# A two-layer graph network on one core: the self part of pass 1's operands turned on VectorE and reloaded, operand products in one batch, moments on ScalarE

## The chip, the core and the metric

The kernel runs on one core of a Trainium2 chip. The metric is the device time of one execution in microseconds. A core has five engines, each with its own instruction queue, which it works off in order: TensorE (PE in the profile; its weight loads are shown apart as PEld), VectorE (DVE), ScalarE (ACT), GpSimd (POOL) and SyncE (SP), which here issues nearly all DMAs. Engines wait for one another by semaphores. Matmuls write to PSUM, eight banks of 2 KB a partition; everything else lies in SBUF.

## The reference

128 graphs of 64 nodes with 768 features pass through two layers, both with a layer norm and a ReLU ahead and a residual sum behind.

```python
# layer 0
h = relu(layernorm(x))
ctx  = (adj @ (h @ Wadj.T + badj)) / deg + (adj.T @ (h @ Wrev.T + brev)) / rdeg + h @ Wself.T + bself
rel  = einsum('bij,bijr->bir', adj, E[rels]) @ Wr.T + br * deg     # here rels = heads = adj
rel += einsum('bij,bijr->bir', adj.T, E[rr]) @ Wrr.T + brr * rdeg
x = x + ctx + rel
# layer 1: graph attention with six heads and a gate
h = relu(layernorm(x))
x = x + gat(h, adj)
```

The relation part is computed as a count of ids in each row, times a small table.

## The kernel before

Two graphs make a tile of 128 rows and two tiles a pair: 32 pairs. Pass 1 computes layer 0 for all pairs, pass 2 layer 1. Everything named below is pass 1 unless it says otherwise. All arithmetic is float32, but for the counts, which are exact in bfloat16.

**Products.** The three dense products of a pair, h normed by the adjacency, by its transpose, and h itself, each by its own 768 x 768 weight, are one product with a contraction of 3 x 768. Rows (2 tiles, `k`), contraction (3 blocks, `q`) and columns (3 blocks) are multiplied by a scheme that needs 15 block products (`PRODUCTS`) where the plain way needs 18 (`PLAIN`, used in pair 0). Its left factors are the operands `a{k}{q}` and their sums `f1` to `f11` (`A_SUMS`), its right factors weight blocks and their sums (`B_SUMS`), which stay in SBUF all through pass 1. A block product is six matmuls of 128 x 128 by 128 x 256: two blocks of 128 (`q`) times three parts (`s`: adjacency, reverse, self). `main` lists these matmuls as steps: 90 for a pair, and one for the last count product. A product ends with an add or subtract of its PSUM bank on VectorE into the x tile (L630, L632), after a product of counts for some (L622). There are four accumulator banks, `pwa` to `pwd`; a bank goes on accumulating after it has been read, so its next product waits for VectorE's read.

**Operands.** `operands(p, k, q)` (L582) makes the transposed left factors of one pair for one `k` and `q`: eight rows of it in the trace are four float32 matmuls with h (64 rows of one graph, 128 columns) as the stationary and `rts` (64 x 192) as the moving side. `rts` holds the scaled adjacency, the scaled transpose, and a third part that is the identity: it turns h without change. Each call fills two banks of the `pb` pool (two buffers of two banks), and ScalarE copies the result to an `op` tile of 128 x 768 (L599). `form` (L602) makes the sums on VectorE.

**Order.** All queues are written out by hand. `merged` walks through the steps of pair p and puts in the side work of `beside(p)` where its number says: the operands of pair p+1 in three batches of two calls (46, 58, 70), its norm (`deviation` L280, `scaled_mean`, `relu`, at 13 and 20), degrees, counts of ids (`ids_worth`, `ids_sum`, `digits`), the sums of operands, the loads of x for p+2 (66), and the end of pair p-1. That end, `finish`, has three parts for each tile: moments of the new x on VectorE; relu, residual sum on POOL, and two stores; transpose in 32 x 32 blocks on VectorE and a store. Pass 2 reads this last store back in 128-byte pieces in such a way that it arrives transposed (`load_h`, L329).

**The seam.** In the last pair `fetch` (L338) loads the weights of layer 1 over those of layer 0 as these come free, loads h of pair 0 (step 30), and makes the weight sums on VectorE. The ends of the last pair are put into the first round of pass 2 (L1203).

Of the kernel before, what the change touches and what calls it, by code (L numbers as in the profile page):

```python
# [15 lines left out]
P = 128  # L16
# [57 lines left out]
               "+", i > 0) for i, q in enumerate((0, 2, 1)) for k in range(2) for j in range(3))  # L74

# [55 lines left out]
def kernel(  # L131
# [86 lines left out]

    H1D = [[dram.tile([KB * P, P], F32, name=f"h1_{p}_{k}") for k in range(2)] for p in range(NP)]
# [52 lines left out]
    def row_constants():  # L272
        nc.sync.dma_start(bb, row(b_att, P))
        nc.vector.tensor_scalar(bb, bb, 1.0, None, op0=OP.add)
        for c in range(3):
            for i in range(NPART):
                a = c * HB + i * H
                nc.sync.dma_start(dl[a : a + H, :], ident[0:H, 0:H])

    def deviation(src, to, mv):  # L280

        st = small.tile([P, 2, 6], F32, name="st")
        for i in range(2):
            nc.vector.bn_stats(st[:, i, :], src[:, i * HALF : (i + 1) * HALF])
        nc.vector.bn_aggr(mv, st.rearrange("p a b -> p (a b)"))
        ve = small.tile([P, 1], F32, name="ve")
        nc.vector.tensor_scalar(ve, mv[:, 1:2], EPS, None, op0=OP.add)  # L287
        nc.gpsimd.tensor_tensor(to[:, 0:1], ve, mhalf, op=OP.pow)  # L288

# [48 lines left out]
    def fetch():  # L338


        def load_block(n):
            j, q = int(n[1]), int(n[2])
            to = bw2[n].rearrange("p (k s n) -> p k s n", k=KQ, s=2)
            for s, src in enumerate((w_cat, hw_t)):
                nc.sync.dma_start(
                    to[:, :, s, :],
                    src.rearrange("(j k p) n -> j p k n", k=KQ, p=P)[j][:, :, q * CQ : (q + 1) * CQ])

        return ([(30, lambda: load_h(0)), (67, lambda: nc.sync.dma_start(hbb, row(hb, P)))]
                + [(i, lambda n=n: load_block(n)) for i, n in (  # L350
                    (7, "b10"), (13, "b00"), (13, "b21"), (25, "b11"), (31, "b01"), (37, "b20"),
                    (49, "b22"), (49, "b02"), (61, "b12"))]
                + [(i, lambda n=n: sum_of_weights(bw2, n)) for i, n in (
                    (22, "g10"), (28, "g6"), (41, "g12"), (46, "u"), (50, "g14"), (57, "w"),
                    (59, "g5"), (65, "v"), (67, "g3"), (70, "g9"), (73, "g1"), (76, "g8"),
                    (79, "g11"))])


    with ExitStack() as px:
# [123 lines left out]
        H0, ADF, AB, CNT, CT_T, GR, WO, SUM, HF = {}, {}, {}, {}, {}, {}, {}, {}, {}  # L483
# [5 lines left out]

        def prep(p):  # L490

            af = ADF[p] = work.tile([P, 2, 2, N], F32, name="af", bufs=1)
            nc.vector.tensor_copy(af, AI[p])
            ab = AB[p] = work.tile([P, 2, 2, N], BF16, name="ab", bufs=1)
            nc.vector.tensor_copy(ab, af)
# [86 lines left out]
        def operands(p, k, q):  # L582


            t = 2 * p + k
            ps = pss.tile([P, GT, 512], F32, name="pb")
            for i in range(2):
                kb = 2 * q + i
                for g in range(GT):
                    s = slice(g * N, (g + 1) * N)  # L590
                    nc.tensor.matmul(ps[:, g, i * 3 * N : (i + 1) * 3 * N],  # L591
                                     H0[t][s, kb * P : (kb + 1) * P],
                                     rts[p % 2][s, k].rearrange("p s n -> p (s n)"),
                                     start=True, stop=True)

            a = OPS[p, f"a{k}{q}"] = (
                work.tile([P, KQ, 3, P], F32, name="oq") if (k, q) == (1, 1) else
                work.tile([P, KQ, 3, P], F32, name="op", bufs=17))
            nc.scalar.copy(a.rearrange("p h s (g n) -> p g (h s) n", g=GT),  # L599
                           ps[:, :, : 6 * N].rearrange("p g (x n) -> p g x n", n=N))  # L600

        def form(p, *names):  # L602

            for n in names:
                s0, x, s1, y = A_SUMS[n]
                t = OPS[p, n] = work.tile([P, KQ, 3, P], F32, name="op", bufs=17)
                signed(t, s0, OPS[p, x], s1, OPS[p, y])

        def main(p):
# [4 lines left out]
            def new(b):  # L614
                bank[b] = psw.tile([P, 512], F32, name=f"pw{b}")
# [18 lines left out]
            def product(an, bn, b, first, c, sign, cnt):  # L634
                def step(q, s):
                    if first and q == s == 0:
                        new(b)
                    nc.tensor.matmul(  # L638
                        bank[b][:, :CQ], OPS[p, an][:, q, s, :],
# [23 lines left out]
        def finish(p, k):  # L663
# [4 lines left out]
            def norm_and_store():  # L668
                scaled_mean(to, mv)
                h = HF[t] = keep.tile([P, D], F32, name="hf", bufs=3)  # L670
                nc.scalar.activation(h, X[t], AF.Relu, scale=to[:, 0:1], bias=to[:, 1:2])  # L671
                nc.gpsimd.tensor_add(X[t], X[t], h)  # L672
                nc.sync.dma_start(of[t * P : (t + 1) * P, :], X[t])
                hh = keep.tile([P, D], F32, name="hh", tag="hf", bufs=3)
                nc.scalar.activation(hh, h, AF.Identity, scale=0.5, bias=half)
                nc.sync.dma_start(HHD[p][k * P : (k + 1) * P, :], hh)

            def turn_and_store():


                ht = keep.tile([P, D], F32, name="ht", tag="hf", bufs=3)
                nc.vector.transpose(ht, HF[t])
                nc.sync.dma_start(H1D[p][k].rearrange("(b p) n -> p b n", p=P),
                                  ht.rearrange("p (b n) -> p b n", b=KB))

            mv = small.tile([P, 2], F32, name="mv")
            return (lambda: deviation(X[t], to, mv), norm_and_store, turn_and_store)
# [31 lines left out]
        operands(0, 0, 0)  # L719
# [3 lines left out]
        operands(0, 0, 1)  # L723
# [3 lines left out]

        def devs(p):
            DEV[p] = deviations((2 * p, 2 * p + 1))

        def relus(p):
            for k in range(2):
                mean_and_relu(2 * p + k, DEV[p][0][k], DEV[p][1][k])

        def degrees_and_norms(p):
            rd = degrees(p)
            relus(p)
            one_over(rd)
            over_degrees(p, rd)

        def weights_sums(*names):
# [7 lines left out]
            (4, lambda: operands(0, 0, 2)),  # L749
            (8, lambda: count(0, 1)),  # L750
            (12, lambda: operands(0, 1, 0)),
            (12, lambda: operands(0, 1, 1)),
            (17, lambda: operands(0, 1, 2)),
# [16 lines left out]
            (54, lambda: operands(1, 1, 2)),  # L770
            (54, lambda: operands(1, 1, 1)),
# [3 lines left out]
            (64, lambda: operands(1, 0, 0)),  # L775
            (64, lambda: operands(1, 0, 2)),
# [3 lines left out]
            (80, lambda: operands(1, 1, 0)),  # L780
            (80, lambda: operands(1, 0, 1)),
# [4 lines left out]
        def beside(p):  # L786


            ends = [f for k in range(2) for f in finish(p - 1, k)]
            steps = [(0, lambda: form(p, "f5", "f6", "f3")), (10, lambda: form(p, "f10")),  # L790
                     (18, lambda: form(p, "f11"))]
            steps += list(zip((32, 40, 44, 49, 55, 59), ends))
            if p == 1:
                steps += [(8, lambda: weights_sums("g9")), (25, lambda: weights_sums("g1"))]
            if p == 3:
                steps += [(74, row_constants)]
            if p + 1 == NP:
                return steps + fetch()
            n = p + 1
            return steps + [  # L800
                (7, lambda: prep(n)),
                (13, lambda: devs(n)),
                (20, lambda: degrees_and_norms(n)),
                (30, lambda: prep_c(n)),
                (37, lambda: ids_worth(n, 0)),
                (43, lambda: ids_sum(n, 0)),
                (46, lambda: operands(n, 1, 2)),
                (46, lambda: operands(n, 1, 1)),
                (53, lambda: form(n, "f1")),
                (56, lambda: ids_worth(n, 1)),  # L810
                (58, lambda: operands(n, 0, 0)),
                (58, lambda: operands(n, 0, 2)),
                (61, lambda: ids_sum(n, 1)),
                (64, lambda: digits(n)),
                (66, lambda: form(n, "f7", "f4")),
                (66, lambda: load(n + 1)),
                (70, lambda: operands(n, 1, 0)),
                (70, lambda: operands(n, 0, 1)),
                (77, lambda: form(n, "f8", "f9", "f2")),
                (80, lambda: count_t(n, 0)),  # L820
                (85, lambda: count_t(n, 1))]

        for p in range(NP):
# [4 lines left out]
    with ExitStack() as px:  # L828
# [374 lines left out]
        ends = [f for k in range(2) for f in finish(NP - 1, k)]  # L1203
        order = parsed(ORDER)
        SUMMED_HERE = (NT - 1,)
        for i in range(min(k for _, k in order), NP - 2):
            if i >= 0:
                load(i + 1)
            for j, (n, k) in enumerate(order):
                if i == 0 and j in (33, 56, 62, 78, 100, 106):  # L1210
                    ends.pop(0)()
# [53 lines left out]
```

## Time and profile before

| | |
|---|---|
| time, median of 3 runs (2452.13 to 2452.39) | 2452.14 us |
| the profiled execution | 2452.42 us |
| its span | 2450.6 us |
| TensorE busy | 2424.8 us |
| VectorE busy | 2047.8 us |
| ScalarE busy | 1025.6 us |
| POOL busy | 449.2 us |
| HBM read, written | 96.07 MB, 100.66 MB |

The page has one line an engine, then the span in 40 slices, then DMA queues, the chain of work that ended last, and the costliest groups of instructions: line, engine, operation, output<-inputs, shapes, count, then busy time, mean of one, and the idle time ahead of them with what ended it. The slices of TensorE, VectorE and the DMA engines show pass 1 in the first 24 and pass 2 after them:

```profile
PE   9999999999999999999999998999999999999997
DVE  8888788788788788788788767789999989888999
DMA  5112212212213113113113146565555555555544
```

In pass 1 a pair repeats every 45.74 us: the transpose of counts of a pair's second tile stands at 803.53 us in the timeline of TensorE and that of the next pair at 849.27. Records of matmuls overlap in the trace, so what a stretch of them takes is read from their starts.

### The profile page before, as it was taken

To read this page: it belongs to the slowest core of one execution; us is meant where nothing else is said; L and a number is where in the kernel's file an instruction comes from. 1 tells how busy PE (TensorE), PEld (TensorE's weight loads), DVE (VectorE), ACT (ScalarE), POOL (GpSimd) and SP (SyncE) were. 2 spreads that over 40 slices of the span, in tenths; PEclk is the share of its full clock that TensorE was granted. 3 is DMA by queue.
4 is the path that set the end of the run, shared out by engine and by line. 5 is a ranking of instruction groups with operands and counts; after the bars stand their busy time and mean duration, and the time that the engine had idled before them with its cause. 6 is when DMAs were issued, how large, how long until landed. Compare 5 with 4: busy or idle time off the path is not lost.

```text
span 2450.6 us, 34880 instructions
## 1 busy us (share of the span) xinstructions
PE 2424.8 (99%) x11777; PEld 1689.8 (69%) x11777; DVE 2047.8 (84%) x4169; ACT 1025.6 (42%) x3399; POOL 449.2 (18%) x799
## 2 busy tenths in 40 slices
PE   9999999999999999999999998999999999999997
PEld 7888888888888888888888885444444444444445
DVE  8888788788788788788788767789999989888999
ACT  2122222222222222122122122776777777777677
POOL 1112112112112112112122112111111111111122
PEclk9999999999999999999999999999999999999999
DMA  5112212212213113113113146565555555555544
GB/s 181 55 54 90 73 54 92 70 55 95 67 54 99 64 54 102 60 54 108 55 55 108 54 115 161 91 119 116 113 109 113 113 108 115 108 107 118 109 98 101
DMA packets 348660, 224.54 MB, mean 92 GB/s; under 512 B 236234, under 2 KB 298813, under 8 KB 348482
## 3 DMA queue, kind: packets, MB, share of 16 engines
q1 hardware_dynamic: 338610, 197.51, 30.0%
q0 software_dynamic: 9728, 24.78, 6.4%
q8 instruction: 92, 1.51, 0.2%
q14 instruction: 86, 0.70, 0.1%
q10 hardware_dynamic: 144, 0.04, 0.0%
HBM read 96.07 MB, written 100.66 MB: 80 GB/s over the span
## 4 chain that ended last, share of the span: by engine, by line
PE 93%; DVE 4%; ACT 1%; DMA 1%; issue 0%; SPq 0%; DVEq 0%; POOL 0%; ACTq 0%; POOLq 0%
PE pwa L638 20%; PE pwb L638 16%; PE pma L908 13%; PE pmb L908 11%; PE pwc L638 7%; PE pwd L638 7%; PE pb L591 6%; PE pmc L908 4%; PE pmd L908 4%; PE ps L1061 2%; PE pwd L622 1%; PE ps L1043 1%; DVE weights L309 1%; ACT pr L960 1%; PE ps L1012 0%
## 5 line engine op out<-in xcount | busy, mean ns | idle before, releaser
L638 PE MATMUL pwa<-weights,op 128*128 128x256 f32 x2304 | 547.7, 382 | 4.1 <-DVE x L630 2.6
L638 PEld LDWEIGHTS pwa<-weights,op 128*128 128x128 f32 x2304 | 420.8, 190 | 66.9 <-issue 7.6
L638 PE MATMUL pwb<-weights,op 128*128 128x256 f32 x1536 | 360.8, 381 | 0.3 <-DVE x L630 0.3
L638 PEld LDWEIGHTS pwb<-weights,op 128*128 128x128 f32 x1536 | 286.6, 190 | 44.4 <-issue 6.7
L908 PE MATMUL pma<-weights,op_f 128*128 128x512 f32 x620 | 310.3, 597 | 1.1 <-DVE weights L935 0.8
L288 POOL TENSOR_TENSOR rn<-ve,mhalf 128x1 f32<-128x1 f32 x128 | 93.5, 730 | 935.4 <-DVE ve L287 935.3
L309 DVE TENSOR_TENSOR op<-op 128x768 f32<-128x768 f32 x248 | 241.4, 993 | 1.2
L960 ACT ACTIVATE pr<-pr 128x128 f32<-128x128 f32 x768 | 225.3, 295 | 25.1 <-DVE pr L950 24.1
L488 ACT ACTIVATE h<-x,rn 128x768 f32<-128x768 f32 x64 | 62.4, 1020 | 383.1 <-DVE rn L292 364.2
L671 ACT ACTIVATE hf<-x,rn 128x768 f32<-128x768 f32 x64 | 65.7, 1027 | 357.6 <-DVE rn L292 349.3
L908 PEld LDWEIGHTS pma<-weights,op_f 128*128 128x128 f32 x620 | 112.2, 190 | 138.7 <-issue 103.2
L599 ACT COPY op<-pb 128x768 f32<-128x768 f32 x160 | 121.1, 797 | 180.0 <-PE pb L591 179.8
L908 PE MATMUL pmb<-weights,op_f 128*128 128x512 f32 x372 | 193.1, 601 | 0.4 <-DVE hz L935 0.4
L638 PE MATMUL pwc<-weights,op 128*128 128x256 f32 x780 | 187.0, 383 | 0.0
L638 PE MATMUL pwd<-weights,op 128*128 128x256 f32 x768 | 176.3, 379 | 0.0
L638 PEld LDWEIGHTS pwc<-weights,op 128*128 128x128 f32 x780 | 145.6, 190 | 25.2 <-issue 6.7
L672 POOL TENSOR_TENSOR x<-x,hf 128x768 f32<-128x768 f32 x64 | 135.7, 2121 | 133.4 <-ACT hf L671 133.4
L638 PEld LDWEIGHTS pwd<-weights,op 128*128 128x128 f32 x768 | 145.8, 190 | 20.0 <-issue 0.2
L591 PE MATMUL pb<-r,h 64*128 64x192 f32 x1536 | 152.0, 337 | 0.4 <-ACT h L488 0.4
L591 PEld LDWEIGHTS pb<-r,h 64*128 64x128 f32 x1536 | 123.0, 187 | 33.9 <-issue 23.0
L960 ACT ACTIVATION_READ_ACCUMULATOR pr<-pr 128x1 f32 x768 | 144.3, 188 | 0.0
L1033 ACT ACTIVATE pb<-al,mx 128x64 f32<-128x64 f32 x384 | 128.5, 337 | 12.4 <-DVE mx L1025 11.6
(210 smaller groups left out, 4143.6 us busy)
## 6 DMA issues: line engine op xcount, KB each, us to landing
x<-in_x_dram SPq DMA_DIRECT2D x64, 384.0 KB
out_dram<-x SPq DMA_DIRECT2D x64, 384.0 KB
hh<-hh SPq DMA_DIRECT2D x64, 384.0 KB
h<-ht SPq DMA_DIRECT2D x64, 384.0 KB
h<-h SPq DMA_DIRECT2D x256, 96.0 KB
x<-hh SPq DMA_DIRECT2D x64, 384.0 KB
out_dram<-f POOLq DMA_DIRECT2D x62, 384.0 KB, 4.7
hx<-weights SPq DMA_DIRECT2D x88, 192.0 KB
```

The lines of the kernel that those rows point to most:

```text
L288: nc.gpsimd.tensor_tensor(to[:, 0:1], ve, mhalf, op=OP.pow)
L309: return (nc.vector.tensor_add if s1 == "+" else nc.vector.tensor_sub)(to, x, y)
L488: nc.scalar.activation(h, X[t], AF.Relu, scale=to[:, 0:1], bias=to[:, 1:2])
L591: nc.tensor.matmul(ps[:, g, i * 3 * N : (i + 1) * 3 * N], H0[t][s, kb * P : (kb + 1) * P], rts[p % 2][s, k].rearrange("p s n -> p (s n)"), ...
L599: nc.scalar.copy(a.rearrange("p h s (g n) -> p g (h s) n", g=GT), ps[:, :, : 6 * N].rearrange("p g (x n) -> p g x n", n=N))
L638: nc.tensor.matmul(bank[b][:, :CQ], OPS[p, an][:, q, s, :], bw[bn][:, (s * KQ + q) * CQ : (s * KQ + q + 1) * CQ], start=(first and q == s ...
L671: nc.scalar.activation(h, X[t], AF.Relu, scale=to[:, 0:1], bias=to[:, 1:2])
L672: nc.gpsimd.tensor_add(X[t], X[t], h)
L908: nc.tensor.matmul(bank[p, b], operand(p, an)[:, q, :], bw2[bn][:, 2 * q * CQ : 2 * (q + 1) * CQ], start=(first and q == 0), stop=(q == KQ ...
L960: nc.scalar.activation(PR[t][:, j, h, :], PR[t][:, j, h, :], AF.Copy, accum_out=to)
L1033: nc.scalar.activation(PB[t][:, h, :], AL[t][:, h, :], AF.Exp, bias=MX[t][:, h : h + 1], accum_out=DN[t][:, h : h + 1])
L1061: nc.tensor.matmul(po[r][o, c, :], PT[t][s, c, o], (hs if r == g else HX[t])[s, 2 * c + r, :], start=True, stop=True)
```

## The change

Nothing changes in the 15 products, the counts or pass 2's own work. Seven things change in pass 1:

1. For pairs from 2 on (`SHARED`) the self part of an operand is not made by a matmul. ScalarE writes the normed h once more with its columns mixed (`relu_mixed`), VectorE transposes it in 32 x 32 blocks (`turn_own`), SP stores it to DRAM (`put_own`), and six DMAs load it transposed into the third part of the operand tiles (`load_own`). The operand matmuls have 128 columns instead of 192, and ScalarE copies 512 elements a partition instead of 768.
2. The six calls of a pair come in one batch (`operands_in_one`) at step 83, over six banks: both `pb` buffers and the banks of c and d, which now are one tile.
3. The moments of these norms and of all ends are two passes on ScalarE with accumulators (`moments`) and three small instructions on POOL (`norm_of`), where two statistics instructions, an aggregate, an addition and a scaled mean ran on VectorE.
4. The casts of the adjacency are on ScalarE, from pair 1 on.
5. Operand tiles have fixed places (`SLOTS`), two sums are made in place (`IN_PLACE`), and their layout has the part outside the block.
6. The side work of `beside` is in smaller pieces in the new order `BESIDE`: f4, f8, f9 and f2 are made in the pair that uses them, loads of the self part stand ahead of the stores of the pair before, and loads of x behind these.
7. At the seam the loads of h of pair 0 move from step 30 to step 62.

```diff
+BESIDE = {"f5": 1, "prep": 1, "dev0": 5, "f4": 8, "dev1": 11, "f8": 12, "deg": 15, "f9": 16,
+          "norm0": 16, "turn0": 17, "f2": 18, "f3": 18, "f6": 19, "put0": 20, "f10": 21,
+          "f11": 25, "norm1": 25, "edev0": 25, "over": 28, "turn1": 32, "enorm0": 32,
+          "rts": 34, "put1": 36, "eturn0": 36, "a11": 38, "a00": 40, "a01": 42, "prepc":
+          43, "esum0": 43, "a12": 45, "a02": 46, "etput0": 49, "edev1": 51, "idw0": 54,
+          "ids0": 54, "idw1": 58, "ids1": 60, "eput0": 62, "enorm1": 62, "esum1": 62,
+          "eput1": 62, "load": 62, "dig": 65, "a10": 70, "ct0": 71, "eturn1": 79, "ct1":
+          82, "etput1": 83, "ops": 83, "f1": 85, "f7": 86}
...
+    def moments(src, by):
+        sums = small.tile([P, 2], F32, name="su")
+        nc.scalar.activation(by, src, AF.Copy, scale=-1.0 / D, accum_out=sums[:, 0:1])
+        nc.scalar.activation(by, src, AF.Square, bias=sums[:, 0:1], accum_out=sums[:, 1:2])
+        return sums
+
+    def norm_of(sums, to):
+        nc.gpsimd.tensor_scalar(to[:, 0:1], sums[:, 1:2], 1.0 / D, EPS, op0=OP.mult, op1=OP.add)
+        nc.gpsimd.tensor_tensor(to[:, 0:1], to[:, 0:1], mhalf, op=OP.pow)
+        nc.gpsimd.tensor_tensor(to[:, 1:2], sums[:, 0:1], to[:, 0:1], op=OP.mult)
...
-        return ([(30, lambda: load_h(0)), (67, lambda: nc.sync.dma_start(hbb, row(hb, P)))]
+        return ([(62, lambda: load_h(0)), (67, lambda: nc.sync.dma_start(hbb, row(hb, P)))]
...
+        def relu_mixed(t, to):
+            hp = HP[t]
+            nc.scalar.activation(
+                hp.rearrange("p (b f i) -> p b f i", b=KB, f=NQ),
+                X[t].rearrange("p (b i f) -> p b f i", b=KB, f=NQ),
+                AF.Relu, scale=to[:, 0:1], bias=to[:, 1:2])
+
+        def turn_own(t):
+            h = HPT[t] = work.tile([P, D], F32, name="hpt", bufs=1)
+            nc.vector.transpose(h, HP[t])
+
+        def put_own(t):
+            nc.sync.dma_start(H0D[t].rearrange("(b p) n -> p b n", p=P),
+                              HPT[t].rearrange("p (b n) -> p b n", b=KB))
...
+        def load_own(p, *names):
+            for n in names:
+                k, q = int(n[1]), int(n[2])
+                nc.sync.dma_start(
+                    new_operand(p, n)[:, 2].rearrange("p b (a n) -> p (b a) n", a=NQ),
+                    H0D[2 * p + k].rearrange("(b i) (f n) -> (i f) b n", i=Q, n=Q)[
+                        :, q * KQ * NQ : (q + 1) * KQ * NQ, :])
...
-        def operands(p, k, q):
-            t = 2 * p + k
-            ps = pss.tile([P, GT, 512], F32, name="pb")
...
+        def operands(p, *calls, last=False):
+            n = 2 if p in SHARED else 3
+            if last:
+                CD.clear()
+                ps = psw.tile([P, GT, 512], F32, name="pwcd")
+            else:
+                ps = pss.tile([P, GT, 512], F32, name="pb")
...
+        def operands_in_one(p):
+            calls = ((1, 2), (1, 1)), ((0, 0), (0, 2)), ((1, 0), (0, 1))
+            ps = [operands(p, *c, last=c is calls[2]) for c in calls]
+            for v, c in zip(ps, calls):
+                operands_out(p, v, *c)
...
+        SHARED = range(2, NP)
...
+                if n in IN_PLACE:
+                    OPS[p, n] = OPS[p, IN_PLACE[n]]
+                else:
+                    new_operand(p, n)
+                signed(OPS[p, n], s0, OPS[p, x], s1, OPS[p, y])
...
-                        bank[b][:, :CQ], OPS[p, an][:, q, s, :],
+                        bank[b][:, :CQ], OPS[p, an][:, s, q, :],
```

In `beside`, a name with `dev`, `norm`, `turn` or `put` belongs to the norm of pair p+1, one with an `e` ahead of it to the end of pair p-1, a name `a..` is a load of a self part, `idw`, `ids`, `dig` and `ct` are the counts, and `ops` is the batch. In the first round of pass 2 the ends of the last pair are put in at the same places as before, with the moments on ScalarE.

## The prediction

> **What bounds the kernel now.** I read the page first (busy shares, the chain of waits, the costly groups), then the busy time by windows, then TensorE's timeline around one batch of operand products, and last the seam between the passes.
>
> ```profile
> PE 2424.8 (99%) x11777; PEld 1689.8 (69%) x11777; DVE 2047.8 (84%) x4169; ACT 1025.6 (42%) x3399; POOL 449.2 (18%) x799
> ...
> PE 93%; DVE 4%; ACT 1%; DMA 1%; issue 0%; SPq 0%; DVEq 0%; POOL 0%; ACTq 0%; POOLq 0%
> ...
> L591 PE MATMUL pb<-r,h 64*128 64x192 f32 x1536 | 152.0, 337 | 0.4 <-ACT h L488 0.4
> ```
>
> The chain is TensorE for 93% of the span. In pass 1 TensorE never idles (the columns are length, then PE, PEld, DVE, ACT, POOL busy):
>
> ```profile
> 600.00:800.00 200.00, 200.00 (x1079) 169.42 (x1078) 161.25 (x326) 50.55 (x72) 39.70 (x37) 1.00 0.25 83
> ```
>
> So pass 1 lasts as long as its matmul stream, and busy VectorE time counts only where TensorE would wait for it. A busy sum overlaps itself (a record of 382 ns starts every 216 ns), so I take times from starts. One batch of two calls of `operands` inside product b:
>
> ```profile
> 824.77 1.89 PE L638 MATMUL pwb<-weights,op 128*128 128x256 f32 x8
> 826.59 1.57 PE L591 MATMUL pb<-r,h 64*128 64x192 f32 x16
> 828.09 1.13 PE L638 MATMUL pwb<-weights,op 128*128 128x256 f32 x4
> 829.06 2.75 PE L638 MATMUL pwd<-weights,op 128*128 128x256 f32 x12
> ```
>
> Twelve records of L638 take 2.59 us (829.06 to the next row, 831.65), 0.216 each; a float32 matmul is two records, so a step of the main list is 0.432 us. From 824.77 to 829.06 are 4.29 us, 2.59 of them the twelve records of L638: the batch costs 1.70 us. Pair 0 has a smaller batch beside a full one:
>
> ```profile
> 17.09 0.92 PE L591 MATMUL pb<-r,h 64*128 64x192 f32 x8
> 17.94 3.72 PE L638 MATMUL pwa<-weights,op 128*128 128x256 f32 x16
> 21.59 1.57 PE L591 MATMUL pb<-r,h 64*128 64x192 f32 x16
> 23.09 2.43 PE L638 MATMUL pwa<-weights,op 128*128 128x256 f32 x10
> ```
>
> Eight more records take 1.50 - 0.85 = 0.65 us, 0.163 for each two: the halves g = 0 and 1 sit on different rows of the array and run together. Sixteen are 8 x 0.163 = 1.30 us, so 0.40 us of each batch goes into changing to 64 rows and back. What 128 columns on 64 rows take is seen in pass 2 (L1061):
>
> ```profile
> 1816.07 0.28 PE L1061 MATMUL ps<-hx,pT 64*64 64x128 f32 x2
> 1816.08 0.36 PE L1061 MATMUL ps<-weights,pT 64*64 64x128 f32 x2
> 1816.17 0.28 PE L1061 MATMUL ps<-hx,pT 64*64 64x128 f32 x2
> ```
>
> A group follows a group after 0.10 to 0.11 us. At the seam VectorE is the bound for a moment:
>
> ```profile
> 1447.12 2.86 PE L638 MATMUL pwa<-weights,op 128*128 128x256 f32 x12 [0.29 <-DVE x L630]
> ...
> 1481.47 4.54 PE L638 MATMUL pwa<-weights,op 128*128 128x256 f32 x12 [2.33 <-DVE x L630]
> ...
> 1490.35 2.86 PE L638 MATMUL pwa<-weights,op 128*128 128x256 f32 x12 [1.52 <-DVE x L632]
> ```
>
> **What the Trainium skill says.** "TensorE: Matmul & The Clock Gate", The mechanism: matmuls of different row groups run at once, and weight loads overlap those of other groups; the trace agrees (0.163 us for two). The same page, LDWEIGHTS: a load takes its columns over 1.2 GHz, whatever the rows; 128 columns are then 107 ns. "TensorEngine Tiling (Array Packing)", Key Properties: a change of tiling mode drains the array; the 0.40 us is what this trace shows of it. "DMA: Bandwidth & Descriptors", Two DMAs through the same engine are not ordered: a reload has to wait for the store's semaphore. No run shown has that in pass 1, but the turned h of layer 1 goes the same way.
>
> **The change part by part.** *Operand products.* For pairs 2 to 31 the columns fall from 192 to 128 and three batches become one: 48 records, 24 twos. Per two, the moving side gives 0.108 (L1061). The load: 187 ns for 128 columns here, 132 for 64 columns in L1061, so 55/64 ns a column, 110 ns for 128 plus a fixed part that overlaps. I take 0.110. New batch 24 x 0.110 + 0.40 = 3.04 us against 3 x 1.70 = 5.10: 2.06 us a pair, 30 pairs, 61.8 us. Bounds: 0.107 gives 64; a load that doesn't overlap, 0.187, gives 24 x 0.187 + 0.40 = 4.89, and 6 us in all. Pairs 0 and 1 keep 192 columns: nothing.
>
> *The batch's own waits.* It begins before step 83 of 91; call that 0. Its third group needs banks c and d, whose last adds come after steps 71 and 53: free. ScalarE's copies fall from 768 to 512 elements a partition (0.80 us now; 640 elements fewer, the copies of L580 at 0.27, give 0.83 ns an element, so 0.59). The first group is ready at about 1.3, six copies end at 4.9; the last count product, in bank d, comes at 3.04 + 7 x 0.432 + 2 x 0.22 = 6.5. Then f7 is wanted at 6.7. On VectorE it is last in a row: the add of product 13 (ready at 3.04 + 0.43 + 0.22 + 0.2 = 3.9, 0.42), f1 and f7 (0.99 each by the page's L309) end at 6.3. Covered, by 0.4 us, the least cover of the new order. f4, f8, f9 and f2, moved behind the start of their own pair, have 3 us and more.
>
> *VectorE.* Per pair go four deviations (two 0.55, 0.21, 0.15, 0.15 us each, 6.4 in all) and two casts (0.58); two transposes come (0.97 each). It gets 5 us lighter. Its densest stretch is steps 54 to 78: four products and sums of ids (2.04 + 1.88, twice), digits 1.0, and between them the adds of f6 and f8. From the add of f11 at 24.1 us of the pair, f6's add ends at 30.8 (wanted at 32.1) and f8's at 33.8 (wanted at 34.7): 0.9 us of cover, so nothing on the path. If that goes, what is late is the b bank of product 13.
>
> *ScalarE and POOL.* The moments add two ScalarE passes to each of four tiles (1.02 us and up to 0.19 for the accumulator, as in L960), the mixed relu two: 12 us a pair beside 12 now, in 43.7: hidden. POOL gets three small instructions (0.73 each, L288) where it had one. The wait this makes is that of the transpose of h (`turn0`, step 17) on moments, POOL and relu: ScalarE reaches `dev0` about 1.1 us before the pair begins, so 1.3, 3.5 after POOL, 4.8 after the mixed relu. VectorE gets there at 8.1 anyway. Queued behind it are f2 and f3, and f3 is wanted at 13.3 and done at 11.2: cover 3.3 + 2.1 = 5.4 us.
>
> *DMA.* A pair stores 2 x 384 KB more and loads 6 x 128 KB in 128-byte pieces; 73 GB/s (400 to 1400 us) over 45.7 us are 3.3 MB now, so 4.9 MB in 43.7 us, 112 GB/s. Pass 2 runs at 111 GB/s with such pieces and TensorE full. On SP the loads of a11, a00, a01, a12 and a02 wait for the second store (issued at about 17.5 us of the pair) and for PE at step 41; they should land near 25, and f1 asks at 41. The x loads stand behind the pair's stores, at about 29, and are read after 42. Hidden.
>
> *The seam.* In the last pair, h of pair 0 (eight DMAs, 4.86 us of SP at 1458.42) no longer stands ahead of the weights b01 and b20, and the stores no longer wait for VectorE's moments. So VectorE's weight sums come some 4 us sooner and no longer pile up at 1478 to 1490. There now go 2.33 + 1.52 us of waiting and 4.54 - 2.75 = 1.8 us of a slower clock after it. I take 4 of these 5.6 us; the unknown (later h loads, four more forms in this pair) makes it 7 gained to 3 lost.
>
> **Sum.** 61.8 + 4 = 66 us. The profiled execution took 2452.42, with a span of 2450.6; the median of the runs is 2452.14, so one sum serves both: 2386 us.
>
> **The rivals.** *A, a thin cover at f7.* VectorE's forms beside POOL have reached 1.1 us in the trace's rows (839.88, two in 2.17), which takes most of the 0.4; with later copies TensorE waits 0.4 us a pair: 12 us back, 2398. For it: the cover is small. Against: before, the same kind of chain never stopped TensorE.
>
> *B, loads don't overlap.* 187 ns for two: only 6 + 4 us gained, 2442. For it: loads and products become equally long, which no batch here shows. Against: the present two take 163 ns with a load of 187.
>
> *C, slower: VectorE stands at the transpose of h.* In order, it holds f2, f3 and all adds behind. The moments are not in this trace. Each us beyond the 5.4 of cover stops TensorE in 30 pairs; past 5.4 + 2.2 = 7.6 us the gain is gone. Nine us late would be 3.6 x 30 = 108 lost, 2494. For it: three engines in a row and x loads behind stores. Against: nothing in the sums above comes near.
>
> That the change does nothing would need pass 1 to be bound by something else, which the full windows exclude.
>
> **How the numbers follow.** Forecast 0.76 (own range 2377 to 2396), A 0.10, B 0.05, C 0.06, 0.03 that gains and waits cancel. The range 2376 to 2404 takes in A. Faster (by over 0.2%, 5 us, what such a measurement can tell) 0.91, same 0.03, slower 0.06.
>
> **What would show it.** Starts of like rows one pair apart (45.74 us now) at about 43.7; L673 rows of 48 records in 2.9 us; no wait of TensorE on VectorE above 0.3 us in steady pairs; the gaps at the seam mostly gone. Rows of L673 at 0.19 a two would mean B, waits at the first L745 rows of a pair A, long VectorE idle before the transpose of `hp` C.

## The result, and the profile after

The changed kernel takes **2620.23 us** (median of 4 runs, 2619.53 to 2622.63) against 2452.17 us for the kernel before beside it: a ratio of 1.0687, with a 95% interval of 1.0668 to 1.0705. It is slower by 168 us; the forecast was 66 us faster. The profiled execution has a span of 2617.8 us and a mean granted TensorE clock of 0.958, as a share of full speed (0.998 before).

The page of after, with busy times, the slices of TensorE and its clock, and the chain that ended last:

```profile
PE 2456.4 (94%) x11777; PEld 1720.5 (66%) x11777; DVE 1988.0 (76%) x3547; ACT 1335.0 (51%) x4017; POOL 520.3 (20%) x1047
...
PE   7999899989989998999899899999999999999997
...
PEclk8999999989998999999899999999999999999999
...
PE 81%; DVE 14%; ACT 1%; DMA 1%; issue 1%; POOL 1%; SPq 0%; DVEq 0%; POOLq 0%; ACTq 0%
```

VectorE's busy time fell and ScalarE's rose, as meant. But VectorE's share of the chain went from 4% to 14%, and in pass 1 both TensorE and its clock have slices below 9. The same 200 us as in the prediction (length, then PE, PEld, DVE, ACT, POOL busy, then PEclk):

```profile
600.00:800.00 200.00, 182.94 (x958) 155.49 (x957) 136.95 (x216) 79.93 (x138) 41.44 (x58) 0.93 0.35 98
```

TensorE, full before, now stands still for 17 of the 200 us, at a mean clock of 0.93. What it waits for, from the waits of TensorE over the whole span (sum, times, longest):

```profile
PE pb L652 <- POOL c L644: 126.9, 30, 4.3
PE pwcd L745 <- DVE x L737: 12.7, 1, 12.7
```

L652 is the transpose of a pair's counts, L644 the copies on POOL that it reads; L745 is a product of the main list, L673 an operand product, L729 a product of counts. One wait in TensorE's timeline, and the batch of operand products behind it:

```profile
830.27 2.32 PE L745 MATMUL pwcd<-weights,op 128*128 128x256 f32 x10
836.86 0.47 PE L652 MATMUL pb<-identb,c 128*126 128x128 bf16 x2 [4.27 <-POOL c L644]
837.13 1.17 PE L745 MATMUL pwcd<-weights,op 128*128 128x256 f32 x2
838.09 0.63 PE L729 MATMUL pwcd<-tab,cntT 126*128 126x256 bf16 x2
838.51 4.97 PE L745 MATMUL pwa<-weights,op 128*128 128x256 f32 x12
...
845.16 0.65 PE L745 MATMUL pwb<-weights,op 128*128 128x256 f32 x2
845.74 2.06 PE L673 MATMUL pb<-r,h 64*128 64x128 f32 x32
847.63 1.06 PE L673 MATMUL pwcd<-r,h 64*128 64x128 f32 x16
848.62 0.70 PE L745 MATMUL pwb<-weights,op 128*128 128x256 f32 x2
849.15 0.39 PE L729 MATMUL pwb<-tab,cntT 126*128 126x256 bf16 x2
```

Three things are to be seen (a product of the main list is twelve records). Ten records from 830.27 end at 832.43 (0.216 each), so the transpose, at 836.86, is 4.43 us late. Then twelve records take 4.81 us (838.51 to the next row at 843.32) instead of 2.59: TensorE runs at about half speed for a while after the wait, called the half clock from here on. And the batch itself costs what was forecast: from 845.16 to 849.15 are 3.99 us, less four records of L745 at 0.216 leaves 3.13 us (3.04 forecast). The steady pair, from one batch to the next, is 51.20 us, against 45.74 before.

Why the copies on POOL are late, from VectorE's timeline of the same pair:

```profile
825.29 0.42 DVE L737 TENSOR_TENSOR x<-pwcd,x 128x256 f32<-128x256 f32 x1 [1.36 <-PE pwcd L729]
825.63 1.01 DVE L616 TENSOR_TENSOR eq<-gr,vals 128x1664 bf16<-128x1664 bf16 x1
826.68 2.52 DVE L619 TENSOR_TENSOR eq<-eq,wo 128x1664 bf16<-128x1664 bf16 x1
829.23 1.89 DVE L624 TENSOR_REDUCE sum<-eq 128x26 f32<-128x1664 bf16 x1
831.15 1.02 DVE L616 TENSOR_TENSOR eq<-gr,vals 128x1664 bf16<-128x1664 bf16 x1
832.21 1.02 DVE L619 TENSOR_TENSOR eq<-eq,wo 128x1664 bf16<-128x1664 bf16 x1
833.15 0.42 DVE L737 TENSOR_TENSOR x<-pwa,x 128x256 f32<-128x256 f32 x1
833.49 1.88 DVE L624 TENSOR_REDUCE sum<-eq 128x26 f32<-128x1664 bf16 x1
...
836.04 0.25 DVE L639 CAST cnt<-di 128x156 bf16<-128x156 int32 x1
836.20 0.41 DVE L739 TENSOR_TENSOR x<-x,pwb 128x256 f32<-128x256 f32 x1
```

and from POOL's:

```profile
825.69 2.63 POOL L781 TENSOR_TENSOR x<-x,hf 128x768 f32<-128x768 f32 x1 [1.14 <-ACT hf L777]
836.42 0.72 POOL L644 COPY c<-cnt 128x243 bf16<-128x243 bf16 x2 [8.10 <-DVE cnt L639]
```

The work on ids of both tiles (two comparisons L616, two products L619, two sums L624) and the digits behind it form one row from 825.63 to 836.2, with one add out of PSUM in it. POOL waits 8.10 us for their end. And the first L619 took 2.52 us where the second took 1.02: it stood beside the residual add on POOL (825.69 to 828.32). So the theory (**T** in the expectations): TensorE waits for counts because their transpose came forward into a stretch of VectorE that ends later than it, and each wait is followed by the half clock. The rivals: something else in the new order also holds TensorE, so that the time stays up when this wait goes (**R**), or the clock falls for another reason.

### The profile page after: what moved, and what is told of

Read it like the earlier page. It is cut to its first block, busy times and chain, and to the rows that moved or that the text cites. A ratio compares the mean times of both kernels' runs of the same rounds, so it can differ in the third digit from the quotient of the medians.

```text
span 2617.8 us, 35645 instructions
## 1 busy us (share of the span) xinstructions
PE 2456.4 (94%) x11777; PEld 1720.5 (66%) x11777; DVE 1988.0 (76%) x3547; ACT 1335.0 (51%) x4017; POOL 520.3 (20%) x1047
## 4 chain that ended last, share of the span: by engine, by line
PE 81%; DVE 14%; ACT 1%; DMA 1%; issue 1%; POOL 1%; SPq 0%; DVEq 0%; POOLq 0%; ACTq 0%
PE pwa L745 18%; PE pwb L745 13%; PE pma L1050 12%; PE pwcd L745 11%; PE pmb L1050 10%; DVE sum L624 4%; PE pmc L1050 4%; DVE eq L619 4%; PE pmd L1050 4%; PE pb L673 2%; DVE eq L616 2%; PE ps L1203 2%; PE pwcd L729 1%; PE pwcd L673 1%; DVE x L737 1%
## 5 line engine op out<-in xcount | busy, mean ns | idle before, releaser
L745 PE MATMUL pwa<-weights,op 128*128 128x256 f32 x2304 | 593.6, 413 | 0.3 <-DVE x L737 0.3
L745 PEld LDWEIGHTS pwa<-weights,op 128*128 128x128 f32 x2304 | 475.7, 212 | 76.4 <-issue 0.9
L745 PE MATMUL pwb<-weights,op 128*128 128x256 f32 x1932 | 455.9, 381 | 0.0
L745 PE MATMUL pwcd<-weights,op 128*128 128x256 f32 x1560 | 384.7, 392 | 12.7 <-DVE x L737 12.7
L745 PEld LDWEIGHTS pwb<-weights,op 128*128 128x128 f32 x1932 | 359.5, 190 | 49.5
L745 PEld LDWEIGHTS pwcd<-weights,op 128*128 128x128 f32 x1560 | 299.8, 196 | 54.2 <-DVE x L737 12.9
L344 DVE TENSOR_TENSOR op<-op 128x768 f32<-128x768 f32 x310 | 326.4, 1070 | 3.9
L315 ACT ACTIVATE hf<-x 128x768 f32<-128x768 f32 x64 | 53.7, 839 | 230.6 <-DVE ht L793 219.8
L652 PE MATMUL pb<-identb,c 128*126 128x128 bf16 (+1 forms) x128 | 23.4, 274 | 127.5 <-POOL c L644 126.9
L737 DVE TENSOR_TENSOR x<-pwb,x 128x256 f32<-128x256 f32 x64 | 27.0, 421 | 148.9 <-PE pwb L729 147.8
L737 DVE TENSOR_TENSOR x<-pwcd,x 128x256 f32<-128x256 f32 x128 | 52.8, 412 | 113.2 <-PE pwcd L729 113.2
L1050 PE MATMUL pmc<-weights,op_f 128*128 128x512 f32 x248 | 129.7, 604 | 0.2 <-DVE weights L1079 0.2
```

The lines of the kernel that those rows point to most:

```text
L315: nc.scalar.activation(by, src, AF.Copy, scale=-1.0 / D, accum_out=sums[:, 0:1])
L344: return (nc.vector.tensor_add if s1 == "+" else nc.vector.tensor_sub)(to, x, y)
L737: nc.vector.tensor_add(v, bank[b][:, :CQ], v)
L745: nc.tensor.matmul(bank[b][:, :CQ], OPS[p, an][:, s, q, :], bw[bn][:, (s * KQ + q) * CQ : (s * KQ + q + 1) * CQ], start=(first and q == s ...
L1050: nc.tensor.matmul(bank[p, b], operand(p, an)[:, q, :], bw2[bn][:, 2 * q * CQ : 2 * (q + 1) * CQ], start=(first and q == 0), stop=(q == KQ ...
```

## The experiments

All but one start from the kernel after. Where only one execution was made, the kernel before, run beside it, took 2452.3 us (the first four), 2453.7 (e7_before_ct0_71, median of seven) or 2454.0 (e8_fill and e9_old_places). The four executions of after span 3.1 us, so single executions are used only for larger differences. Diffs of `BESIDE` show only the entries that change.

**The transpose later (e1_ct0_late).**

```diff
-"ct0": 71
+"ct0": 81
```

> The changed kernel with one number altered: the transpose of the counts of the pair's first tile (ct0) goes into TensorE's order at step 81 instead of 71. Theory T (TensorE stands at this transpose because the counts on VectorE and the copies on POOL behind it are late, 4.3 us a pair, and runs at half clock for 6 us after it, 3.1 us more): the wait goes, about 1 us is left at product 13, whose bank waits for the add of f8 behind the counts; a pair falls from 51.2 to about 44.7 us, the whole to about 2425 us (2395 to 2440). Rival R (VectorE's queue as a whole is too slow in the new order, and the transpose is only where it shows first): the same wait comes back at product 13 or at f7, the time stays at 2600 to 2620.

Measured: 2430.36 us, clock 0.996. One number in a table takes 190 us back, and the kernel is now faster than before. The pair is 44.81 us. Without any wait it would be 43.72, as e5_all shows below; in TensorE's timeline the rest is seen at product 13 (bank b) and at the one ahead of it (bank a):

```profile
836.43 2.86 PE L745 MATMUL pwa<-weights,op 128*128 128x256 f32 x12 [0.38 <-DVE x L737]
839.47 1.56 PE L745 MATMUL pwb<-weights,op 128*128 128x256 f32 x6 [0.18 <-DVE x L739]
```

They wait for the adds of f6 and f8, to which the prediction gave 1.3 and 0.9 us of cover. The first L619 takes 2.52 us in this run too, and these 1.5 us are more than either cover. It costs about 1 us a pair: small, beside the transpose. So R is there too, but with only 1 of the 7.5 us by which a pair of after exceeds 43.72.

**The count work earlier (e2_counts_early).**

```diff
-"idw0": 54, "ids0": 54, "idw1": 58, "dig": 65
+"idw0": 48, "ids0": 48, "idw1": 54, "dig": 60
```

> The changed kernel with the counts on VectorE some steps earlier (idw0 and ids0 at 48 instead of 54, idw1 at 54 instead of 58, digits at 60 instead of 65), the transpose still at step 71. Theory T: the counts no longer stand behind the add of product f11, their chain ends 2.7 us sooner, so the wait at the transpose falls from 4.3 to about 1.6 us; if the clock stays up after so short a wait, a pair takes about 45.4 us and the whole about 2450 us, if it still falls, about 2530. Rival R: VectorE has the same work, so the wait reappears at another bank and the time stays above 2590.

Measured: 2440.81 us, clock 0.996, pair 45.14 us. T holds, from the other side: the transpose stays at 71 and its input comes sooner. TensorE's timeline:

```profile
842.21 0.33 PE L652 MATMUL pb<-identb,c 128*126 128x128 bf16 x2 [1.19 <-POOL c L644]
842.38 0.65 PE L745 MATMUL pwcd<-weights,op 128*128 128x256 f32 x2
842.86 0.39 PE L729 MATMUL pwcd<-tab,cntT 126*128 126x256 bf16 x2
843.09 2.75 PE L745 MATMUL pwa<-weights,op 128*128 128x256 f32 x12
```

The rows behind a wait of 1.19 us are at full speed. The edit does a second thing: the digits now stand ahead of the second residual add in POOL's queue, so that add comes later (at 842.45), and every L619 takes 1.02 us. So this gain has two parts, the earlier places and the freed L619.

**POOL's add gone (e3_no_residual_add).**

```diff
-nc.gpsimd.tensor_add(X[t], X[t], h)
```

> The changed kernel without the residual sum x + h of layer 1 on POOL in pass 1 (its output lacks that h). Theory that POOL's add holds VectorE up (the product of eq and wo takes 2.52 us beside it instead of 1.02, f11 2.23 instead of 0.95): both fall back to about 1.0, the chain of counts ends 1.5 us sooner, the wait at the transpose falls from 4.3 to 2.8 us, and 30 pairs give 45 to 65 us: 2555 to 2575. If the long instruction has another cause, nothing moves: 2620.

Measured: 2535.28 us, clock 0.975. In VectorE's timeline L619 takes 1.02 us and the f11 form (L344), 2.23 us in after beside the other add, takes 0.95:

```profile
825.19 0.95 DVE L344 TENSOR_TENSOR op<-op 128x768 f32<-128x768 f32 x1
...
837.54 1.02 DVE L619 TENSOR_TENSOR eq<-eq,wo 128x1664 bf16<-128x1664 bf16 x1
```

The wait is 2.77 us, 1.5 less than the 4.27 of after, which is L619's share; what f11 gains is mostly lost again, as VectorE then waits 2.26 us instead of 1.36 for TensorE ahead of the add at L737. The gain of 85 us is more than the expected 45 to 65: 1.5 us in 30 pairs are 45, and a shorter wait also keeps more of the clock (0.975 against 0.958).

**Pair 0 over three banks (e4_banks_pair0).**

```diff
-"abcdab"[2 * i + k]
+"abcabc"[2 * i + k]
```

> The changed kernel with the banks of pair 0's plain products in the order a b c a b c instead of a b c d a b. Theory that the 12.7 us wait in pair 0 comes from c and d being one tile now, so that the products into d wait for VectorE's add out of c, which stands behind weight sums and counts: the wait goes, pair 0 takes about 48 us from its degrees to those of the next instead of 61.6, the whole about 2606. Rival (pair 0 is bound by VectorE's queue anyway): the wait moves on to another bank, 2615 to 2620.

Measured: 2607.49 us. The 12.7 us of the second row of waits are this: c and d are now one tile, so pair 0's first product into d waits until VectorE has read c, and that read stands behind weight sums and count work (in after it comes at 57.30 us, and TensorE goes on at 57.77).

**The kernel before with the transpose at 71 (e7_before_ct0_71).**

```diff
-(80, lambda: count_t(n, 0)),
+(71, lambda: count_t(n, 0)),
```

> The kernel before with one edit: its first transpose of counts at step 71 instead of 80. If the step number alone makes the loss, TensorE waits some 4 us a pair here too, with the half clock behind it, and the time is near 2600 us. If the loss needs the new surroundings (two batches of 1.70 us gone from between steps 46 and 71, and the four weight and sum operations packed from steps 37 to 61 into 54 to 60), the copies on POOL end at 841.25 of the profile, before step 71 (about 842), so that at most a short wait for a pb buffer stays: 2452 to 2465 us.

Measured: 2452.56 us, nothing lost. TensorE's timeline has no wait at the transpose (L577 here), and POOL's copies (L569) end at 840.20, 1.5 us ahead of it:

```profile
839.67 1.57 PE L591 MATMUL pb<-r,h 64*128 64x192 f32 x16
841.17 0.70 PE L638 MATMUL pwc<-weights,op 128*128 128x256 f32 x2
841.70 0.28 PE L577 MATMUL pb<-identb,c 128*126 128x128 bf16 x2
```

```profile
838.75 1.45 POOL L569 COPY c<-cnt 128x243 bf16<-128x243 bf16 x2 [3.42 <-DVE cnt L564]
```

So the step number alone does no harm; the loss needs the rest of the new order.

**The count work at its old places (e9_old_places).**

```diff
-"prepc": 43, "idw0": 54, "ids0": 54, "idw1": 58, "ids1": 60, "dig": 65
+"prepc": 30, "idw0": 37, "ids0": 43, "idw1": 56, "ids1": 61, "dig": 64
```

> The kernel after with the count work at the steps it had in the kernel before (products and sums of ids at 37, 43, 56, 61, digits at 64, the counts' preparation at 30), while the transpose of counts stays at 71. If packing this work into steps 54 to 60 is what made the digits late, TensorE's wait at the transpose is under 1 us, the clock stays up, and the time is 2390 to 2435 us (pair 0's 12 us are still lost). If it is enough that two batches of operand products no longer stand between steps 46 and 71, the wait stays above 2 us and the time above 2500 us.

Measured: 2512.86 us, clock 0.984, a wait of 1.85 us. The wait lies between the two expectations; the time, with the half clock in it, is in the range of the second. Spreading the count work takes 2.4 of the 4.27 us away, so packing it is over half of the lateness. The rest is not packing: L616 now meets POOL's add (2.45 us instead of 1.01), and no batches stand between steps 46 and 71 any more. How these two share the rest wasn't taken apart.

This run shows the clock best. Two pairs in a row in TensorE's timeline, with the same wait:

```profile
783.22 0.33 PE L652 MATMUL pb<-identb,c 128*126 128x128 bf16 x2 [1.85 <-POOL c L644]
784.09 2.75 PE L745 MATMUL pwa<-weights,op 128*128 128x256 f32 x12
...
829.75 0.33 PE L652 MATMUL pb<-identb,c 128*126 128x128 bf16 x2 [1.85 <-POOL c L644]
...
830.62 4.44 PE L745 MATMUL pwa<-weights,op 128*128 128x256 f32 x12
```

After the first the clock stays up, after the second it falls. Of 29 pairs 11 take about 46.5 us (one of them 46.9) and 18 take 48.2.

**The wait filled (e8_fill).**

```diff
...
+if k == 0 and p in SHARED:
+    for _ in range(10):
+        nc.tensor.matmul(pt[:, 1, :CQ], ident, bw["b00"][:, :CQ], start=True, stop=True)
```

> The kernel after with ten float32 products of 128 x 128 by 128 x 256 put on TensorE ahead of each pair's first transpose of counts (pairs 2 to 31), into an unused half of its pb tile; nothing reads them. At 0.432 us each they fill 4.3 us, the length of the wait. If the half clock behind the wait comes from TensorE's idleness, rows keep 0.216 us spacing, the wait shrinks to nearly nothing, and the time falls by 30 x 3.1 = 93 us to about 2527 us (2515 to 2545). If the slower clock has another cause (a throttle by load), the products come on top or the clock stays down: 2600 us or more.

Measured: 2533.78 us, clock 0.996. Here `pt` is the transpose's own pb tile, in the half that nothing reads. The filling stands in TensorE's timeline where the wait was, and the rows behind it are at full speed (here lines are four further on: L651 the filling, L656 the transpose, L749 products):

```profile
841.77 4.48 PE L651 MATMUL pb<-weights,ident 128*128 128x256 f32 x20
846.20 0.32 PE L656 MATMUL pb<-identb,c 128*126 128x128 bf16 x2
846.36 0.65 PE L749 MATMUL pwcd<-weights,op 128*128 128x256 f32 x2
846.85 0.39 PE L733 MATMUL pwcd<-tab,cntT 126*128 126x256 bf16 x2
847.07 2.75 PE L749 MATMUL pwa<-weights,op 128*128 128x256 f32 x12
```

The transpose comes 4.43 us late as in after (841.77 to 846.20), and only the clock differs. So the fallen clock is worth 2620.2 - 2533.8 = 86 us, or 2.9 us a pair, and it comes from TensorE standing still.

**Together (e5_all).** The edits of e1, e2 and e4.

> The kernel after with three edits together: the transpose of counts at step 81 instead of 71, the products of weights and counts of ids six steps earlier, and pair 0 over banks a, b, c only. If the wait of the count transpose, the half clock behind it and pair 0's bank d are all that the changed order lost, the pair falls to 43.74 us (45.74 less 2.0 of the batch) and the time to 2452 - 60 - 4 of the seam = 2388 us (2383 to 2398). If another loss was hidden behind the wait (a later bank, ScalarE's copies, POOL's queue), TensorE shows a new wait in each pair and the time stays above 2400.

Measured: **2385.47 us** (4 runs, 2384.94 to 2386.02), ratio to before 0.9725, interval 0.9710 to 0.9739. The windows view shows pass 1 full again, with more ScalarE beside it than before (97.93 us, 50.55 then):

```profile
600.00:800.00 200.00, 200.00 (x1100) 173.44 (x1099) 155.30 (x257) 97.93 (x163) 49.27 (x76) 1.00 0.39 106
```

The pair is 43.72 us. No wait of TensorE returns in each pair; POOL's copies end at 850.77, 2.9 us ahead of the transpose at 853.67.

**The h loads at the seam (e6_h_loads_30).** Like e5_all, with

```diff
-(62, lambda: load_h(0))
+(30, lambda: load_h(0))
```

> e5_all with the loads of h of pair 0 at the seam put back from step 62 to step 30. Pass 1's steady pairs are as in e5_all. If the later h loads are what took the seam's gaps away, the old gaps come back and this is 3 to 4 us slower than e5_all. If the gaps went because VectorE no longer makes the moments, it is within 1 us of e5_all.

Measured: 2385.27 us (2384.82 to 2385.82): the same as e5_all. From the last degree product to the first product of pass 2 both take 78.79 us, with one wait of 0.29 us in the last pair, so the place of these loads has no part in the gain at the seam.

## Why the prediction was wrong, by its own steps

**Where the 168 us come from.** The batch, -2.0 us a pair, 30 pairs: -61. The late transpose, 4.43 each: +133. The half clock (e8_fill against after): +86. Pair 0: +12.7. The seam: -4. The sum is +167. The first, second and last term are worked out from traces, the other two are differences of runs (e4_banks_pair0 for pair 0).

**Operand products: right.** 3.13 us against 3.04 forecast, and the pair without waits is 2.02 us shorter (45.74 less the 43.72 of e5_all; 2.06 forecast). Rival B had the batch at 4.89, so it is out.

**The batch's own waits: right.** No steady pair of any run has a wait at f7; rival A's place is free in all of them.

**VectorE: the step that failed.** It says of the densest stretch "0.9 us of cover, so nothing on the path", and that if that goes, "what is late is the b bank of product 13". The sum under it looks at the adds only. It has no line for the other reader of that stretch, the transpose of counts, which the change moves from step 80 to 71: products and sums of ids, then digits, then POOL's copies, then TensorE. On the prediction's own clock (add of f11 at 24.1, which is 825.29 here) the add of f8 ends at 33.8, so the digits, just ahead of it, at about 33.4 and the first copy 0.6 us later. TensorE gets to the transpose at 832.43, or 31.2. The plan's own numbers thus had the transpose about 2.8 us late before anything ran over; e1_ct0_late and e2_counts_early show that this reader is what stops TensorE.

**A term mis-sized in the same step.** The sum has the work on ids at its length in the kernel before, and rival A takes forms beside POOL at "1.1 us" (the POOL instruction of that row is the copy of counts at 839.80, not the residual add). Beside POOL's add they took 2.52 instead of 1.02 (L619) and 2.23 instead of 0.95 (f11), and e3_no_residual_add brings both back. With L619's 1.5 us the plan's 2.8 become the 4.3 of the row. The named b bank is late too, as e1_ct0_late shows, with bank a ahead of it: about 1 us a pair for both.

**What a wait costs.** Only the seam's sum prices the clock behind a wait (4.54 - 2.75 = 1.8 us); rival C, the one account of waits in steady pairs that ends slower, counts a late us as one us. The clock is 86 of the 168 us.

**ScalarE, POOL and DMA hidden: right.** In e5_all TensorE is full with all of this beside it. One size was off without harm: the mixed relu took 1.79 us (mean of L531 in after), where the sum has about the 1.0 of a plain one.

**Pair 0: missed.** "Pairs 0 and 1 keep 192 columns: nothing" looks at the columns and not at the banks. Two banks in one tile became one thing to wait for (e4_banks_pair0).

**The seam: right in size, wrong in one reason.** In after, from the last pair's degree product to pass 2's first product, the stretch grew by 1.8 us (84.50 to 86.27) where a pair had grown by 5.5: 3.7 us gained, 4 forecast. In e5_all it fell by 5.7, 2.02 of which is the batch: 3.7 again. The later h loads were named as one cause, and e6_h_loads_30 excludes them. The other, moments no longer on VectorE, is argued only.

**Rival C: the right kind at the wrong place.** A slower kernel through VectorE's order was the rival on the other side, put at the transpose of h. That one never stands: VectorE reaches it with its input there (809.21 us in after, no wait). The same mechanism, TensorE held by VectorE's order, began 16 us later in the pair, with the work on ids at 825.63.

With the two omissions mended, and the work on ids earlier so that it no longer meets POOL's add, the plan gives what was forecast for it: 2385.5 us against 2386. That doesn't make the forecast right: the order as written was the change.

## What to carry to other kernels

When a consumer is moved forward, list everything that reads the stretch it is moved over, on every engine, and put the time at which each is wanted beside the time at which it is ready; a cover worked out for one reader says nothing of the next. Price a wait of TensorE with the clock that it may lose, which here was two thirds of the wait again; filling the wait with idle products won that part back. Where one place in an order costs 190 us more than one ten steps on, try two or three places before judging the idea.

## What the runs showed of the hardware

**The clock falls after shorter stops than expected, and not after each.** The Trainium skill, "TensorE: Matmul & The Clock Gate", Part 1, has the clock halved after an idle window of about 3.4 us, of a monitor that runs free. The runs fit the free-running window: one and the same stop of 1.85 us costs a pair 0 or 1.7 us (e9_old_places), and 1.7 us is 3.4 us at half clock. Nor does the slow stretch begin with the end of the stop: behind the transpose at 829.75 the records run at full speed up to 830.62. A stop of 2.77 us makes pairs of 46.7, 48.2 to 48.4 or 49.7 us (e3_no_residual_add), which is 0, about 1.7 or 3.0 us of clock. The runs differ from the page on the threshold: 1.85 us is enough in 18 pairs of 29. A stop of 1.2 us cost no clock (e2_counts_early), and one of 4.27 us about 3 us in each steady pair. Where between these the limit lies, and what the monitor counts, isn't shown.

**VectorE against POOL.** The Trainium skill, "SBUF — State Buffer", Who interferes with whom, says that a VectorE instruction with two SBUF inputs contends with a POOL instruction that reads SBUF, through a shared read interface. Their lengths here are those of two that take turns, in the order of their starts. In the kernel before, VectorE's product of ids started first, kept its 1.02 us, and POOL's add, 1.81 us alone (e2_counts_early, 842.45), became the longer one:

```profile
833.53 1.02 DVE L544 TENSOR_TENSOR eq<-eq,wo 128x1664 bf16<-128x1664 bf16 x1
833.76 2.47 POOL L672 TENSOR_TENSOR x<-x,hf 128x768 f32<-128x768 f32 x1 [1.45 <-ACT hf L671]
```

In after the add came between two such instructions: it ended 1.68 us after the first (L616, 826.64), and the second (L619) ended 0.88 us after the add. So that product lost 1.5 us, and the sum f11 1.28 in the same way. Where a sum over ids, with one SBUF input, overlaps the add, neither is longer: in the kernel before one at 826.54 took 1.88 us and the add at 827.49 took 1.82.
